# A convolution kernel's engine queues written directly, with one semaphore for all stores and an ending without barriers

## The chip, the cores and the metric

The kernel runs on one core of a Trainium2 chip. The metric is the device time of one execution in microseconds (us). The profile shows a part of it, the *span*, from the program's first instruction to its last. The timed runs list their own spans (all but the first six of the kernel before), so time minus span can be worked out run by run. I call it the *part outside the span*. Most spans are listed to 0.1 us, so this part is good to 0.05 us in a single run. All runs quoted are listed as fast, that is, none is in the slower state in which some runs of a kernel take some per cent longer.

Some words that return: a *semaphore* is a counter that engines and transfers raise and on which an engine can wait. A *barrier* makes engines wait for each other. A *drain* is an instruction that stands ahead of each barrier here. A transfer raises its semaphore in 16 completions (the trace shows 16 for each); it has *landed* with the last of them. The *tail* is the time from the last landing to the end of the span.

## The reference

The input has 8 images of 32 channels and 128 x 128 pixels in float32. The output is `x + conv(groupnorm(x))`, with a 3 x 3 convolution written as an FFT and cut so that only a shifted corner of it is not plain bias:

```python
def reference(x, L0_conv_weight, L0_conv_bias):
    ...
    fx = jnp.fft.fft2(px, norm='ortho')
    fout = jnp.einsum('bihw,oihw->bohw', fx, wf)
    sp = jnp.fft.ifft2(fout, norm='ortho').real
    sh = (fft_H - out_h) // 2
    out = sp[:, :, sh:sh + out_h, sw:sw + out_w]
    ...
    x = x + _L0_conv_ref(_gn(x), L0_conv_weight, L0_conv_bias, 1, 1)
    return x
```

For the timing it is enough to know that 16.8 MB are read and 16.8 MB are written.

## The kernel before

All of x stays on the core, in four tiles of two images each. SyncE issues nine loads and seven stores through one queue. The kernel is written with a framework that keeps track of tiles, gives out semaphores, places the waits, and ends the program by itself when its context is left. These are the parts that the change and the argument touch; cuts are marked.

```python
    pairs = [xpool.tile([P, 2, H, W], F32, name=f"x{pair}") for pair in range(NPAIR)]
    ...
    for img in range(2):
        for half in range(2):
            rows = slice(half * H // 2, (half + 1) * H // 2)
            nc.sync.dma_start(xts[img][:, rows, :], x[0, :, img, rows, :])
            ...
    for pair in range(2, NPAIR):
        nc.sync.dma_start(pairs[pair], x[pair])
    ...
    for img in range(B):
        ...
        if img:
            add(img - 1, 0, NCHUNK)
            if img == 2 or img == 4:
                nc.sync.dma_start(out[img // 2 - 1], pairs[img // 2 - 1])
            elif img > 4:
                store(img - 1, 0, H)
        ...
    store(B - 1, N, H)
    add(B - 1, 0, 2)
    add(B - 1, 2, NCHUNK)
    store(B - 1, 0, N)
...
    with tile.TileContext(nc) as tc, tc.manual_schedule():
        conv_preact_kernel(tc, *args)
```

No line of the source says how the program ends. Leaving the context (L288 in the profile) makes SyncE wait for every semaphore. Then all engines meet in a barrier, GpSimd clears the semaphores, and all engines meet in a second barrier.

## Time and profile before

| what | before | where it is read |
|---|---|---|
| time | 85.69 us (85.48 to 85.76) | three runs |
| profiled run | 85.45 us, span 83.73, so 1.72 outside | its own time and trace |
| 16 DMA engines busy | 95.3% of the span, 99.3% of 2.5 to 82 us | DMA view |
| TensorE busy | 77%, done at 73.5 us | page and timeline |
| last store landed | 82.90 us | semaphore records |
| from there to the end of the span | 0.83 us | the same |

In these numbers the core is a pipe for bytes. It has a short head and a short tail, and the computation lies beside the transfers. The lines themselves are in the prediction.

### The profile page before, as it was taken

To read this page: it belongs to the slowest core of one execution; us is meant where nothing else is said; L and a number is where in the kernel's file an instruction comes from. 1 tells how busy PE (TensorE), PEld (TensorE's weight loads), DVE (VectorE), ACT (ScalarE), POOL (GpSimd) and SP (SyncE) were. 2 spreads that over 40 slices of the span, in tenths; PEclk is the share of its full clock that TensorE was granted. 3 is DMA by queue.
4 is the path that set the end of the run, shared out by engine and by line. 5 is a ranking of instruction groups with operands and counts; after the bars stand their busy time and mean duration, and the time that the engine had idled before them with its cause. 6 is when DMAs were issued, how large, how long until landed. Compare 5 with 4: busy or idle time off the path is not lost.

```text
span 83.7 us, 734 instructions
## 1 busy us (share of the span) xinstructions
PE 64.6 (77%) x214; PEld 39.4 (47%) x214; DVE 54.5 (65%) x103; ACT 51.8 (62%) x102; POOL 2.3 (3%) x8
## 2 busy tenths in 40 slices
PE   0000998999999999999999999999999999900000
PEld 0000441666666666666666666666666666500000
DVE  0329936991999699699969969996996330070000
ACT  6019427984995798499679849967984993000000
POOL 6400000000000000000000000000000000000000
PEclk9999999999999999999999999999999999995555
DMA  2899999999998999899898999899989999999970
GB/s 43 325 407 419 423 450 427 438 431 415 501 501 344 407 501 415 376 438 493 266 485 376 407 470 501 360 407 485 438 352 399 462 407 454 423 446 388 431 335 20
DMA packets 2211, 33.63 MB, mean 402 GB/s; under 512 B 256, under 2 KB 288, under 8 KB 416
## 3 DMA queue, kind: packets, MB, share of 16 engines
q1 hardware_dynamic: 2208, 33.60, 95.3%
q8 instruction: 1, 0.02, 0.1%
q14 instruction: 2, 0.02, 0.1%
HBM read 16.82 MB, written 16.78 MB: 401 GB/s over the span
## 4 chain that ended last, share of the span: by engine, by line
PE 75%; DMA 8%; ACT 2%; DVE 2%; SPq 1%; issue 1%; DVEq 1%
PE ps L189 69%; DMA x<-x_dram 8%; PE ps_w L214 4%; PE ps_m L148 1%; DVE x L198 1%; ACT g L165 1%; DVEq L288 1%; SPq L71 0%; SPq L69 0%; ACT std L160 0%; ACT square L156 0%; ACT rstd L163 0%; DVE rstd L162 0%; DVE var L157 0%
## 5 line engine op out<-in xcount | busy, mean ns | idle before, releaser
L189 PE MATMUL ps<-g,w_sb 128*128 128x363 f32 (+1 forms) x192 | 58.7, 462 | 0.3 <-ACT g L165 0.3
L189 PEld LDWEIGHTS ps<-g,w_sb 128*128 128x128 f32 x192 | 35.2, 189 | 21.2 <-issue 1.9
L129 DVE BATCH_NORM_STATS2 stats<-x 128x6 f32<-128x512 f32 x64 | 38.7, 676 | 2.5 <-DMA x<-x_dram 2.4
L174 ACT ACTIVATE x<-x,bs_sb 128x1984 f32<-128x1984 f32 x8 | 15.6, 1949 | 0.3
L198 DVE SCALAR_TENSOR_TENSOR x<-ps,bs_sb,x 128x1089 f32<-128x1089 f32 (+2 forms) x9 | 10.5, 1179 | 7.2 <-PE ps L189 7.2
L165 ACT ACTIVATE g<-x,rstd 128x396 f32<-128x396 f32 (+1 forms) x16 | 12.6, 837 | 0.3
L214 PE MATMUL ps_w<-x,avg 128*128 128x512 f32 x6 | 5.8, 1100 | 8.5 <-DMA x<-x_dram 8.5
L176 ACT ACTIVATE x<-x,bs_sb 128x1023 f32<-128x1023 f32 x8 | 9.1, 1133 | 0.0
L214 PEld LDWEIGHTS ps_w<-x,avg 128*128 128x128 f32 x6 | 1.7, 326 | 9.6 <-issue 9.6
L156 ACT ACTIVATE square<-ps_m 128x7 f32<-128x7 f32 x8 | 1.4, 176 | 5.5 <-PE ps_m L148 5.5
L139 ACT ACTIVATE terms<-bs_sb,mv 128x8 f32<-128x8 f32 x8 | 2.4, 301 | 3.8 <-DVE mv L137 3.8
L157 DVE COPY var<-ps_m 128x1 f32<-128x1 f32 x8 | 1.3, 158 | 4.9 <-ACT square L156 4.9
L148 PEld LDWEIGHTS ps_m<-terms,avg 128*128 128x128 f32 x16 | 3.2, 205 | 2.7 <-ACT terms L140 1.2
L160 ACT ACTIVATE std<-var 128x1 f32<-128x1 f32 x8 | 2.4, 295 | 1.8 <-DVE var L157 1.8
L163 ACT ACTIVATE rstd<-ps_m,rstd 128x1 f32<-128x1 f32 x8 | 2.1, 261 | 1.8 <-DVE rstd L162 1.8
L162 DVE RECIPROCAL rstd<-std 128x1 f32<-128x1 f32 x8 | 1.3, 164 | 2.9 <-ACT std L160 2.9
L118 ACT ACTIVATE bs_sb<-wb_sb 32x9 f32<-32x9 f32 x4 | 0.8, 211 | 3.8 <-DMA wb_sb<-wb_dram 3.8
L137 DVE BATCH_NORM_AGGREGATE mv<-stats 128x2 f32<-128x48 f32 x8 | 3.0, 372 | 0.3
L121 ACT ACTIVATE w_sb<-wb_sb 32x64 f32<-32x64 f32 (+2 forms) x16 | 2.8, 244 | 0.0
L148 PE MATMUL ps_m<-terms,avg 128*128 128x9 f32 x16 | 2.5, 226 | 0.0
L140 ACT ACTIVATE terms<-mv,eps 128x1 f32<-128x1 f32 x8 | 2.2, 279 | 0.0
L100 ACT ACT_TABLE_LOAD x1 | 1.3, 1283 | 0.8 <-PEq L281 0.8
(14 smaller groups left out, 5.1 us busy)
## 6 DMA issues: line engine op xcount, KB each, us to landing
x<-x_dram SPq DMA_DIRECT2D x2, 4096.0 KB, 33.8
out_dram<-x SPq DMA_DIRECT2D x2, 4096.0 KB, 16.5
out_dram<-x SPq DMA_DIRECT2D x3, 2048.0 KB, 10.2
x<-x_dram SPq DMA_DIRECT2D x4, 1024.0 KB, 7.7
x<-x_dram SPq DMA_DIRECT2D x2, 2048.0 KB, 17.3
out_dram<-x SPq DMA_DIRECT2D x1, 1056.0 KB, 7.9
out_dram<-x SPq DMA_DIRECT2D x1, 992.0 KB, 11.5
wb_sb<-wb_dram SPq DMA_DIRECT2D x1, 40.5 KB, 4.8
```

Source lines behind the costliest of these rows:

```text
L121: nc.scalar.activation(w6[to, dr, dc, r, c, :], taps[:, a, b, :], AF.Identity)
L129: nc.vector.bn_stats(stats[img][:, s, :], xts[img][:, STATS * s : STATS * (s + 1), :].rearrange("p h w -> p (h w)"),)
L137: nc.vector.bn_aggr(mv, stats[img].rearrange("p n s -> p (n s)"))
L139: nc.scalar.activation(terms[:, 0:NSIGN], signs, AF.Identity, scale=mv[:, 0:1])
L148: nc.tensor.matmul(ps_ms[img], avg, mvs[img], start=True, stop=True)
L160: nc.scalar.activation(std, var[:, 0:1], AF.Sqrt, bias=var[:, 1:2])
L165: nc.scalar.activation(g[:, rows, :], xt[:, LO + rows.start : LO + rows.stop, LO:W], AF.Identity, bias=rstd[:, 1:2], scale=rstd[:, 0:1],)
L174: nc.scalar.activation(low, low, AF.Identity, bias=bias_sb)
L176: nc.scalar.activation(right, right, AF.Identity, bias=bias_sb)
L189: nc.tensor.matmul(ps[:, 0:rows, 0 : N - dc], w_sb[:, k * P : (k + 1) * P], g[:, top : top + rows, dc:N], start=(k == 0), stop=(k == 3),)
L198: nc.vector.scalar_tensor_tensor(part.rearrange("p (n r) w -> p n r w", r=ROWS), in0=pss[img][:, first:last, 0 : ROWS * N].rearrange("p n ...
L214: nc.tensor.matmul(ps_w, avg, piece, start=True, stop=True)
```

## The change

The intent is to keep every computing instruction and its order, and to drop what the framework adds. Each engine has one semaphore, which counts its marked instructions. Each load has its own semaphore, and all stores share one. A small class remembers what each engine has already waited for, and leaves out the waits that follow from others. SyncE's wait for the seven stores ends the program. The core of the diff, cut:

```diff
-    with tile.TileContext(nc) as tc, tc.manual_schedule():
-        conv_preact_kernel(tc, *args)
+    conv_preact_kernel(nc, *args)
...
+    def __call__(self, name, emit, *needs, mark=False, adds=None):
+        engine, seen = self.names[name], self.seen[name]
+        waits = {}
+        for token, of in needs:
+            if seen.get(of, 0) < token[of]:
+                waits[of] = max(waits.get(of, 0), token[of])
...
+        for of, value in waits[:-1]:
+            engine.wait_ge(self.sems[of], value)
+        op = emit(engine)
...
-        nc.sync.dma_start(out[img // 2, :, img % 2, first:last, :], xts[img][:, first:last, :])
+    put.semaphore("stored")
+    def store(to, of, *needs):
+        return put("sp", lambda sp: sp.dma_start(to, of), *needs, adds="stored")
...
+    nc.sync.wait_ge(put.sems["stored"], put.done["stored"])
+    numbers = sorted(sem.num for sem in put.sems.values())
+    nc.sync.sem_clear(range(numbers[0], numbers[-1] + 1))
```

More of the change, by code (lines that the diff above doesn't have):

```diff
@@ L18 @@
-from contextlib import ExitStack
 import concourse.bass as bass
-import concourse.tile as tile
 from concourse import mybir
-from concourse._compat import with_exitstack
 F32 = mybir.dt.float32
@@ L34, with __init__, semaphore, _learn @@
 NSIGN = 8
-@with_exitstack
-def conv_preact_kernel(
-    ctx: ExitStack,
-    tc: tile.TileContext,
-    x: bass.AP,
-    wb: bass.AP,
-    out: bass.AP,
-):
-    nc = tc.nc
+LANDED = 16
+class Queues:
+    def __init__(self, nc):
+        self.nc = nc
+        self.names = {"pe": nc.tensor, "dve": nc.vector, "act": nc.scalar, "pool": nc.gpsimd, "sp": nc.sync}
+        self.sems = {}
+        self.done = {}
+        self.seen = {name: {} for name in self.names}
+        for name in self.names:
+            if name != "sp":
+                self.sems[name] = nc.alloc_semaphore(f"done_{name}")
+                self.done[name] = 0
+    def semaphore(self, name):
+        self.sems[name] = self.nc.alloc_semaphore(name)
+        self.done[name] = 0
+    def _learn(self, name, token):
+        for of, value in token.items():
+            self.seen[name][of] = max(self.seen[name].get(of, 0), value)
+    def __call__(self, name, emit, *needs, mark=False, adds=None):
[4 more added lines that the diff above has]
+                waits[of] = max(waits.get(of, 0), token[of])
+        for token, of in needs:
+            self._learn(name, token)
+        waits = list(waits.items())
+        for of, value in waits[:-1]:
+            engine.wait_ge(self.sems[of], value)
+        op = emit(engine)
+        if waits:
+            of, value = waits[-1]
+            op.wait_op(self.sems[of], value, "sem-ge")
+        if adds is not None:
+            of, by = adds, LANDED
+        elif mark:
+            of, by = name, 1
+        else:
+            return None
+        op.then_inc(self.sems[of], by)
+        self.done[of] += by
+        return {**seen, of: self.done[of]}, of
+def conv_preact_kernel(nc: bass.Bass, x: bass.AP, wb: bass.AP, out: bass.AP):
     NPAIR, _, _, H, W = x.shape
@@ L54, in conv_preact_kernel @@
     NSTAT = H // STATS
-    cpool = ctx.enter_context(tc.tile_pool(name="const", bufs=1))
-    xpool = ctx.enter_context(tc.tile_pool(name="x", bufs=1))
-    spool = ctx.enter_context(tc.tile_pool(name="small", bufs=2))
-    ps_conv = ctx.enter_context(tc.tile_pool(name="ps_conv", bufs=2, space=bass.MemoryType.PSUM))
-    ps_stat = ctx.enter_context(tc.tile_pool(name="ps_stat", bufs=1, space=bass.MemoryType.PSUM))
-    pairs = [xpool.tile([P, 2, H, W], F32, name=f"x{pair}") for pair in range(NPAIR)]
@@ L64, in conv_preact_kernel, with sbuf, psum @@
-    xts = [pairs[img // 2][:, img % 2] for img in range(B)]
-    wb_sb = cpool.tile([C, 9 * C + 4 * (1 + NSIGN)], F32, name="wb_sb")
+    def sbuf(name, *shape):
+        return nc.alloc_sbuf_tensor(name, list(shape), F32).ap()
+    def psum(name, *shape):
+        return nc.alloc_psum_tensor(name, list(shape), F32).ap()
+    put = Queues(nc)
+    pairs = [sbuf(f"x{pair}", P, 2, H, W) for pair in range(NPAIR)]
+    xts = [pairs[img // 2][:, img % 2] for img in range(B)]
+    wb_sb = sbuf("wb_sb", C, 9 * C + 4 * (1 + NSIGN))
@@ L66, in conv_preact_kernel, with load @@
+    loaded = {}
+    def load(to, of):
+        name = f"load{len(put.sems)}"
+        put.semaphore(name)
+        return put("sp", lambda sp: sp.dma_start(to, of), adds=name)
     for img in range(2):
+        loaded[img] = []
         for half in range(2):
             rows = slice(half * H // 2, (half + 1) * H // 2)
-            nc.sync.dma_start(xts[img][:, rows, :], x[0, :, img, rows, :])
+            loaded[img].append((rows.stop, load(xts[img][:, rows, :], x[0, :, img, rows, :])))
             if img == 0 and half == 0:
-                nc.sync.dma_start(wb_sb, wb)
+                weights_in = load(wb_sb, wb)
@@ L72, in conv_preact_kernel @@
     for img in range(2):
-        nc.sync.dma_start(xts[2 + img], x[1, :, img])
+        loaded[2 + img] = [(H, load(xts[2 + img], x[1, :, img]))]
     for pair in range(2, NPAIR):
-        nc.sync.dma_start(pairs[pair], x[pair])
-    pair = cpool.tile([P, P // 2, 2], F32, name="pair")
-    nc.gpsimd.memset(pair, 0.125)
-    nc.gpsimd.affine_select(
-        out=pair, in_=pair, pattern=[[-2, P // 2], [0, 2]], base=0,
-        channel_multiplier=1, compare_op=ALU.is_ge, fill=0.0,
-    )
-    nc.gpsimd.affine_select(
-        out=pair, in_=pair, pattern=[[2, P // 2], [0, 2]], base=1,
-        channel_multiplier=-1, compare_op=ALU.is_ge, fill=0.0,
-    )
@@ L88, in conv_preact_kernel @@
-    w_sb = cpool.tile([P, 4 * P], F32, name="w_sb")
-    nc.gpsimd.memset(w_sb, 0.0)
-    eps = cpool.tile([P, 1], F32, name="eps")
-    nc.vector.memset(eps, EPS * FFT * FFT)
-    pair2 = pair.rearrange("p a b -> p (a b)")
-    avg = cpool.tile([P, P], F32, name="avg")
-    nc.vector.tensor_add(avg[:, 0 : 2 * C], pair2[:, 0 : 2 * C], pair2[:, 2 * C : 4 * C])
-    nc.vector.tensor_add(avg[:, 2 * C : 3 * C], avg[:, 0:C], avg[:, C : 2 * C])
-    for k in (0, 1, 3):
-        nc.vector.tensor_copy(avg[:, k * C : (k + 1) * C], avg[:, 2 * C : 3 * C])
@@ L99, in conv_preact_kernel, with rows_in @@
-    warm = cpool.tile([P, 1], F32, name="warm")
-    nc.scalar.activation(warm, eps, AF.Sqrt)
-    bs_sb = cpool.tile([P, 1 + NSIGN], F32, name="bs_sb")
+        loaded[2 * pair] = loaded[2 * pair + 1] = [(H, load(pairs[pair], x[pair]))]
+    def rows_in(img, last):
+        return [token for k, (_, token) in enumerate(loaded[img]) if k == 0 or loaded[img][k - 1][0] < last]
+    pair = sbuf("pair", P, P // 2, 2)
+    w_sb = sbuf("w_sb", P, 4 * P)
+    eps = sbuf("eps", P, 1)
+    avg = sbuf("avg", P, P)
@@ new lines, in conv_preact_kernel @@
+    warm = sbuf("warm", P, 1)
+    pair_ok = put("pool", lambda e: e.memset(pair, 0.125), mark=True)
+    for step, base in ((-1, 0), (1, 1)):
+        pair_ok = put(
+            "pool",
+            lambda e: e.affine_select(
+                out=pair, in_=pair, pattern=[[2 * step, P // 2], [0, 2]], base=base,
+                channel_multiplier=-step, compare_op=ALU.is_ge, fill=0.0,
+            ),
+            pair_ok, mark=True,
+        )
+    w_zero = put("pool", lambda e: e.memset(w_sb, 0.0), mark=True)
@@ new lines, in conv_preact_kernel @@
+    eps_ok = put("dve", lambda e: e.memset(eps, EPS * FFT * FFT), mark=True)
+    pair2 = pair.rearrange("p a b -> p (a b)")
+    sums = put(
+        "dve", lambda e: e.tensor_add(avg[:, 0 : 2 * C], pair2[:, 0 : 2 * C], pair2[:, 2 * C : 4 * C]),
+        pair_ok, mark=True,
+    )
+    sums = put(
+        "dve", lambda e: e.tensor_add(avg[:, 2 * C : 3 * C], avg[:, 0:C], avg[:, C : 2 * C]), sums, mark=True
+    )
+    for k in (0, 1, 3):
+        avg_ok = put(
+            "dve", lambda e: e.tensor_copy(avg[:, k * C : (k + 1) * C], avg[:, 2 * C : 3 * C]), sums, mark=True
+        )
@@ L105, in conv_preact_kernel @@
+    put("act", lambda e: e.activation(warm, eps, AF.Sqrt), eps_ok)
+    bs_sb = sbuf("bs_sb", P, 1 + NSIGN)
     bias_sb, signs = bs_sb[:, 0:1], bs_sb[:, 1:]
@@ L112, in conv_preact_kernel @@
     }
-    for rin in range(2):
-        for cin in range(2):
-            q = 2 * rin + cin
-            to = slice(q * C, (q + 1) * C)
-            of = 9 * C + q * (1 + NSIGN)
-            nc.scalar.activation(bs_sb[to, :], wb_sb[:, of : of + 1 + NSIGN], AF.Identity)
-            for dr, r, a in places[rin]:
-                for dc, c, b in places[cin]:
-                    nc.scalar.activation(w6[to, dr, dc, r, c, :], taps[:, a, b, :], AF.Identity)
-    gs = [cpool.tile([P, N, N], F32, name=f"g{k}") for k in range(2)]
@@ L124, in conv_preact_kernel, with spread @@
-    stats = [cpool.tile([P, NSTAT, 6], F32, name=f"stats{img}") for img in range(B)]
-    mvs, ps_ms, pss = {}, {}, {}
-    def take_stats(img, first, last):
-        for s in range(first, last):
-            nc.vector.bn_stats(
-                stats[img][:, s, :],
-                xts[img][:, STATS * s : STATS * (s + 1), :].rearrange("p h w -> p (h w)"),
+    def spread(to, of):
+        return put("act", lambda e: e.activation(to, of, AF.Identity), weights_in, w_zero, mark=True)
+    for q in range(4):
+        rin, cin = q // 2, q % 2
+        to = slice(q * C, (q + 1) * C)
+        of = 9 * C + q * (1 + NSIGN)
+        bias_ok = spread(bs_sb[to, :], wb_sb[:, of : of + 1 + NSIGN])
+        for dr, r, a in places[rin]:
+            for dc, c, b in places[cin]:
+                w_ok = spread(w6[to, dr, dc, r, c, :], taps[:, a, b, :])
@@ new lines, in conv_preact_kernel @@
+    gs = [sbuf(f"g{k}", P, N, N) for k in range(2)]
+    stats = [sbuf(f"stats{img}", P, NSTAT, 6) for img in range(B)]
+    mvs = [sbuf(f"mv{k}", P, 2) for k in range(B)]
+    terms = [sbuf(f"terms{k}", P, NSIGN + 1) for k in range(B)]
+    squares = [sbuf(f"square{k}", P, NSIGN - 1) for k in range(B)]
+    variances = [sbuf(f"var{k}", P, 2) for k in range(B)]
+    stds = [sbuf(f"std{k}", P, 1) for k in range(B)]
+    rstds = [sbuf(f"rstd{k}", P, 2) for k in range(B)]
+    pss = [psum(f"ps{k}", P, NCHUNK, BANK) for k in range(2)]
@@ new lines, in conv_preact_kernel, with take_stats @@
+    ps_ms = psum("ps_m", P, BANK)
+    ps_w = psum("ps_w", P, BANK)
+    stats_ok, terms_ok, group_ok, means_read, normal, conv_ok, biased, added = {}, {}, {}, {}, {}, {}, {}, {}
+    warm_ok = None
+    def take_stats(img):
+        for s in range(NSTAT):
+            stats_ok[img] = put(
+                "dve",
+                lambda e: e.bn_stats(
+                    stats[img][:, s, :],
+                    xts[img][:, STATS * s : STATS * (s + 1), :].rearrange("p h w -> p (h w)"),
+                ),
+                *rows_in(img, STATS * (s + 1)), mark=s == NSTAT - 1,
@@ L132, in take_stats @@
             )
     def aggregate(img):
-        mv = spool.tile([P, 2], F32, tag="mv", name=f"mv{img}")
-        nc.vector.bn_aggr(mv, stats[img].rearrange("p n s -> p (n s)"))
-        terms = spool.tile([P, NSIGN + 1], F32, tag="terms", name=f"terms{img}")
-        nc.scalar.activation(terms[:, 0:NSIGN], signs, AF.Identity, scale=mv[:, 0:1])
-        nc.scalar.activation(
-            terms[:, NSIGN:], mv[:, 1:2], AF.Identity, bias=eps, scale=float(FFT * FFT)
-        )
-        mvs[img] = terms
@@ L145, in group @@
-    def group(img):
-        ps_ms[img] = ps_stat.tile([P, NSIGN + 1], F32, tag="ps_m", name=f"ps_m{img}")
-        nc.tensor.matmul(ps_ms[img], avg, mvs[img], start=True, stop=True)
-    def normalize(img):
-        xt, g, ps_m = xts[img], gs[img % 2], ps_ms[img]
-        contrasts = ps_m[:, 1:NSIGN]
-        square = spool.tile([P, NSIGN - 1], F32, tag="square", name=f"square{img}")
-        var = spool.tile([P, 2], F32, tag="var", name=f"var{img}")
-        nc.scalar.activation(square, contrasts, AF.Square, accum_out=var[:, 0:1])
-        nc.vector.tensor_copy(var[:, 1:2], ps_m[:, NSIGN:])
-        std = spool.tile([P, 1], F32, tag="std", name=f"std{img}")
-        nc.scalar.activation(std, var[:, 0:1], AF.Sqrt, bias=var[:, 1:2])
-        rstd = spool.tile([P, 2], F32, tag="rstd", name=f"rstd{img}")
-        nc.vector.reciprocal(rstd[:, 0:1], std)
-        nc.scalar.activation(rstd[:, 1:2], ps_m[:, 0:1], AF.Identity, scale=rstd[:, 0:1])
-        for rows in (slice(0, ROWS + 1), slice(ROWS + 1, N)):
-            nc.scalar.activation(
-                g[:, rows, :], xt[:, LO + rows.start : LO + rows.stop, LO:W], AF.Identity,
-                bias=rstd[:, 1:2], scale=rstd[:, 0:1],
@@ new lines, in aggregate @@
+        mv, t = mvs[img], terms[img]
+        mv_ok = put(
+            "dve", lambda e: e.bn_aggr(mv, stats[img].rearrange("p n s -> p (n s)")), stats_ok[img], mark=True
+        )
+        put("act", lambda e: e.activation(t[:, 0:NSIGN], signs, AF.Identity, scale=mv[:, 0:1]), mv_ok, bias_ok)
+        terms_ok[img] = put(
+            "act",
+            lambda e: e.activation(t[:, NSIGN:], mv[:, 1:2], AF.Identity, bias=eps, scale=float(FFT * FFT)),
+            mark=True,
+        )
+    def group(img):
+        group_ok[img] = put(
+            "pe",
+            lambda e: e.matmul(ps_ms[:, 0 : NSIGN + 1], avg, terms[img], start=True, stop=True),
+            terms_ok[img], avg_ok, *means_read.get(img - 1, ()), mark=True,
+        )
@@ new lines, in normalize @@
+    def normalize(img):
+        xt, g, var, std, rstd = xts[img], gs[img % 2], variances[img], stds[img], rstds[img]
+        square_ok = put(
+            "act",
+            lambda e: e.activation(squares[img], ps_ms[:, 1:NSIGN], AF.Square, accum_out=var[:, 0:1]),
+            group_ok[img], mark=True,
+        )
+        copied = put(
+            "dve", lambda e: e.tensor_copy(var[:, 1:2], ps_ms[:, NSIGN : NSIGN + 1]), square_ok, mark=True
+        )
+        std_ok = put(
+            "act", lambda e: e.activation(std, var[:, 0:1], AF.Sqrt, bias=var[:, 1:2]), square_ok, copied, mark=True
+        )
+        rstd_ok = put("dve", lambda e: e.reciprocal(rstd[:, 0:1], std), std_ok, mark=True)
+        shift_ok = put(
+            "act",
+            lambda e: e.activation(rstd[:, 1:2], ps_ms[:, 0:1], AF.Identity, scale=rstd[:, 0:1]),
+            rstd_ok, mark=True,
+        )
+        means_read[img] = (copied, shift_ok)
+        normal[img] = []
+        for rows in (slice(0, ROWS + 1), slice(ROWS + 1, N)):
+            normal[img].append(
+                put(
+                    "act",
+                    lambda e: e.activation(
+                        g[:, rows, :], xt[:, LO + rows.start : LO + rows.stop, LO:W], AF.Identity,
+                        bias=rstd[:, 1:2], scale=rstd[:, 0:1],
+                    ),
+                    shift_ok, *rows_in(img, H), *conv_ok.get(img - 2, ()), mark=True,
+                )
@@ L173, in add_bias @@
         low = xt[:, N:H, :].rearrange("p h w -> p (h w)")
-        nc.scalar.activation(low, low, AF.Identity, bias=bias_sb)
         right = xt[:, 0:N, N:W]
-        nc.scalar.activation(right, right, AF.Identity, bias=bias_sb)
+        free = [*normal[img]] + ([warm_ok] if img == 0 else [])
+        biased[img] = [
+            put("act", lambda e: e.activation(part, part, AF.Identity, bias=bias_sb), *free, mark=True)
+            for part in (low, right)
+        ]
     def multiply(img, n):
         g = gs[img % 2]
-        if n == 0:
-            pss[img] = ps_conv.tile([P, NCHUNK, BANK], F32, tag="ps", name=f"ps{img}")
-        ps = pss[img][:, n, 0 : ROWS * N].rearrange("p (r w) -> p r w", w=N)
+        ps = pss[img % 2][:, n, 0 : ROWS * N].rearrange("p (r w) -> p r w", w=N)
         for k in range(4):
@@ L188, in multiply, with finished @@
             top = n * ROWS + dr
-            nc.tensor.matmul(
-                ps[:, 0:rows, 0 : N - dc], w_sb[:, k * P : (k + 1) * P],
-                g[:, top : top + rows, dc:N],
-                start=(k == 0), stop=(k == 3),
+            needs = [w_ok, normal[img][min(n, 1)]] + added.get(img - 2, [])
+            ok = put(
+                "pe",
+                lambda e: e.matmul(
+                    ps[:, 0:rows, 0 : N - dc], w_sb[:, k * P : (k + 1) * P],
+                    g[:, top : top + rows, dc:N],
+                    start=(k == 0), stop=(k == 3),
+                ),
+                *needs, mark=k == 3,
             )
+        conv_ok[img] = [ok]
     def add(img, first, last):
-        part = xts[img][:, first * ROWS : last * ROWS, 0:N]
-        nc.vector.scalar_tensor_tensor(
-            part.rearrange("p (n r) w -> p n r w", r=ROWS),
-            in0=pss[img][:, first:last, 0 : ROWS * N].rearrange("p n (r w) -> p n r w", w=N),
-            scalar=bias_sb, in1=part.rearrange("p (n r) w -> p n r w", r=ROWS),
-            op0=ALU.add, op1=ALU.add,
-        )
-    def store(img, first, last):
-        nc.sync.dma_start(out[img // 2, :, img % 2, first:last, :], xts[img][:, first:last, :])
-    ps_w = ps_stat.tile([P, BANK], F32, tag="ps_w", name="ps_w")
+        part = xts[img][:, first * ROWS : last * ROWS, 0:N].rearrange("p (n r) w -> p n r w", r=ROWS)
+        ps = pss[img % 2][:, first:last, 0 : ROWS * N].rearrange("p n (r w) -> p n r w", w=N)
+        ok = put(
+            "dve",
+            lambda e: e.scalar_tensor_tensor(part, in0=ps, scalar=bias_sb, in1=part, op0=ALU.add, op1=ALU.add),
+            *conv_ok[img], bias_ok, mark=True,
+        )
+        added.setdefault(img, []).append(ok)
+    put.semaphore("stored")
+    def store(to, of, *needs):
+        return put("sp", lambda sp: sp.dma_start(to, of), *needs, adds="stored")
+    def finished(*imgs):
+        return [token for img in imgs for token in (*biased[img], *added[img])]
     def keep_warm(first, times):
@@ L213, in keep_warm @@
         for _ in range(times):
-            nc.tensor.matmul(ps_w, avg, piece, start=True, stop=True)
+            ok = put(
+                "pe", lambda e: e.matmul(ps_w, avg, piece, start=True, stop=True),
+                avg_ok, *rows_in(0, H), mark=True,
+            )
+        return ok
     keep_warm(H // 2, 2)
-    take_stats(0, 0, NSTAT)
+    take_stats(0)
     aggregate(0)
     group(0)
-    keep_warm(0, 1)
+    warm_ok = keep_warm(0, 1)
     normalize(0)
     add_bias(0)
-    take_stats(1, 0, NSTAT)
+    take_stats(1)
     for img in range(B):
@@ L232, in conv_preact_kernel @@
             if img == 2 or img == 4:
-                nc.sync.dma_start(out[img // 2 - 1], pairs[img // 2 - 1])
+                store(out[img // 2 - 1], pairs[img // 2 - 1], *finished(img - 2, img - 1))
             elif img > 4:
-                store(img - 1, 0, H)
+                store(out[(img - 1) // 2, :, (img - 1) % 2], xts[img - 1], *finished(img - 1))
         if more:
@@ L241, in conv_preact_kernel @@
         if img + 2 < B:
-            take_stats(img + 2, 0, NSTAT)
-    store(B - 1, N, H)
+            take_stats(img + 2)
+    xt, to = xts[B - 1], out[NPAIR - 1, :, 1]
+    store(to[:, N:H, :], xt[:, N:H, :], biased[B - 1][0])
     add(B - 1, 0, 2)
     add(B - 1, 2, NCHUNK)
-    store(B - 1, 0, N)
+    stored = store(to[:, 0:N, :], xt[:, 0:N, :], biased[B - 1][1], *added[B - 1])
+    seen = {**put.seen["sp"]}
+    for of, value in stored[0].items():
+        seen[of] = max(seen.get(of, 0), value)
+    assert all(seen.get(of, 0) == done for of, done in put.done.items()), (seen, put.done)
+    nc.sync.wait_ge(put.sems["stored"], put.done["stored"])
+    numbers = sorted(sem.num for sem in put.sems.values())
+    assert numbers == list(range(numbers[0], numbers[0] + len(numbers)))
+    nc.sync.sem_clear(range(numbers[0], numbers[-1] + 1))
 def kernel(x, L0_conv_weight, L0_conv_bias):
```

## The prediction

> **What bounds the kernel now.** I read the page first, then the DMA view of the long middle stretch, then the lines of the program's first and last barrier, then when each store was issued and landed. The page's header, its DMA rows and its account of the end:
>
> ```profile
> span 83.7 us, 734 instructions
> PE 64.6 (77%) x214; PEld 39.4 (47%) x214; DVE 54.5 (65%) x103; ACT 51.8 (62%) x102; POOL 2.3 (3%) x8
> ...
> PE   0000998999999999999999999999999999900000
> ...
> DMA  2899999999998999899898999899989999999970
> ...
> q1 hardware_dynamic: 2208, 33.60, 95.3%
> ...
> HBM read 16.82 MB, written 16.78 MB: 401 GB/s over the span
> ```
>
> TensorE has no idle slice from the seventh to its last, and the chain of waits gives it 75% of the span; that looks like the bound. But TensorE is done at 73.5 us of 83.7, and the DMA row is full to the last slice but one. Cut to the stretch from 2.5 to 82 us, the DMA view says it more sharply:
>
> ```profile
> DMA packets 2189, 33.47 MB, mean 421 GB/s; under 512 B 253, under 2 KB 285, under 8 KB 413
> ...
> q1 hardware_dynamic: 2186, 33.44, 99.3%
> ```
>
> The 16 DMA engines are 99.3% busy with the kernel's own loads and stores. So the bound is 33.6 MB through one queue, in order: a head before the first byte moves, some 80 us of transfer, and a tail after the last store has landed. TensorE counts only if it makes a store late. The stores, in the views of their two lines:
>
> ```profile
> L206 SPq DMA_DIRECT2D out_dram<-x x5: 332/332/332, 56.7 to 75.0; - x5
> ...
> DMA to landing us min/median/max: 7.9/10.2/11.6
> ...
> L233 SPq DMA_DIRECT2D out_dram<-x x2: 343/345/347, 34.7 to 49.4; - x2
> ...
> DMA to landing us min/median/max: 14.1/16.5/19.0
> ```
>
> The last store is issued at 75.0 us and lands 7.9 later, at 82.9 us, though its 1.06 MB need only 1.06 / 0.43 = 2.5 us at the rate of the middle: it stands in the queue behind the store before it, which the trace's semaphore records land at 80.39. Each store has such a reserve (issue against landing of the transfer ahead): 34.71 and 44.03, 49.38 and 53.74, 56.70 and 63.44, 64.04 and 68.30, 67.79 and 73.15, 68.86 and 78.01, 75.03 and 80.39. The smallest is 4.3 us. Some of it is the delay before a DMA's first byte, which the start shows as below 2 us (issue at 0.80, and the second slice, which ends at 4.2, already at 8 tenths), so compute may slip by some 2 us before the queue runs dry.
>
> What lies behind the last landing is the program's final barrier (L288):
>
> ```profile
> L288 SPq EVENT_SEMAPHORE  x8: 17/28/28, 75.4 to 83.7; - x8
> L288 POOLq EVENT_SEMAPHORE  x4: 17/17/17, 83.1 to 83.6; - x4
> ...
> L288 SPq DRAIN  x3: 7/7/7, 83.0 to 83.3; - x3
> ...
> L288 POOLq EVENT_SEMAPHORE_RANGE_CLEAR  x1: 96/96/96, 83.3 to 83.3; - x1
> ```
>
> In the single instructions: the last landing at 82.90; SyncE's last wait for it 82.92 to 82.95; its drains at 82.99 and 83.04; GpSimd gathers and releases a first barrier at 83.07 and 83.15; the engines leave it about 83.2, drain, GpSimd clears the semaphores at 83.35 and drains at 83.47; a second barrier is gathered at 83.55 and released at 83.63; the last engine leaves at 83.73. That is 83.73 - 82.90 = 0.83 us in which nothing of the problem is done.
>
> **What the Trainium skill says.** "DMA: Bandwidth & Descriptors", section "Anatomy of one DMA — SWDGE (gpsimd) path", gives the variable cost as bytes over 436 GB/s and calls the fixed cost mostly the wait for the write receipt. The middle runs at 421, so I take the 80 us as not to be shortened by any bookkeeping. The same page, "Why a DMA increments its semaphore by 16 and not by 1", warns that two transfers in flight on one semaphore cannot be told apart by partial counts. The new kernel waits only for the sum of all seven stores, 112, and gives each load its own semaphore, so this is sound and needs no extra wait. "Perfetto Trace Analysis", section "Per-engine timelines", says that a sequencer-only instruction shows only its execution, not its wait or the spread of its update. The trace agrees: SyncE's, GpSimd's and the others' instructions of the tail are 7 to 96 ns each, but their handshakes fill 0.83 us; so the tail has to be read from starts, not from durations. "Runtime: NRT & Kernel Launch", section "Instruction fetch mechanics", says that sequencers fetch their streams by DMA of their own, mostly hidden; I come back to that.
>
> **The change, part by part.**
> (1) Tail. Removed: SyncE's waits for each DMA semaphore in turn (all but the last three are passed without waiting, and those three follow the landings), five drains on the path, two barriers through GpSimd. Left: one wait for 112 on the shared semaphore, and one range clear, now on SyncE. The wait still starts 0.02 after the last landing and takes 0.03 (82.95); the next instruction follows 0.04 later, as the first drain does now; the clear takes 0.10, as on GpSimd: 83.09. Saved: 83.73 - 83.09 = 0.64 us, all on the path, since nothing runs beside it.
> (2) Head. The first barrier (L281) stays. The branch into the kernel's block goes. From the end of SyncE's barrier wait (0.73) to its first load (0.80) are 0.065 us; elsewhere SyncE follows a wait with a DMA after 0.037. Saved: 0.03 us, on the path.
> (3) Loads. The last load waits for a semaphore of the first in order to reuse it (1.1 us, issued at 5.85 instead of about 4.75). It gets its own now. Six transfers stand ahead of it, so its data move when they did. Saved: 0.
> (4) Waits of the engines. The instructions that compute are the same in the same order; in the built programs the semaphore-only instructions fall from 18 to 8 on TensorE and from 18 to 7 on SyncE, and rise from 10 to 12 on ScalarE. Small tiles get a buffer per image, so no wait for reuse is added. All of it lies in the reserve of over 2 us before each store. Saved or lost: 0.
> Sum: 0.64 + 0.03 = 0.67 us; 85.69 - 0.67 = 85.02 us, 0.8%.
>
> **The rivals.**
> (a) The measured time is longer than the span: 85.45 against 83.73 in the profiled run, 1.72 us that no view shows. If part of it is what each engine does after its program, four engines now do it early, and only SyncE after the last landing. For it: the final barrier makes all five end together at 83.7. Against: SyncE still has its own share to do, and if that is the longest nothing is gained. It could take off another 0 to 0.5 us: 84.5 to 85.0.
> (b) Instruction fetches. The trace has two of 8 KB at 32 us and one of 16 KB at 39 us:
>
> ```profile
> q8 instruction: 1, 0.02, 0.1%
> q14 instruction: 2, 0.02, 0.1%
> ```
>
> They look like nothing, but they share the DMA engines. The 16 completions of the last load before them come within 0.5 us (22.65 to 23.16). At 32 us two of the 16 trail by 0.5 us and more; from then on three do, and at the end twelve have landed by 81.81 and the last four at 82.26, 82.35, 82.69 and 82.90. The store ends with its slowest engine, so fetches may cost up to 82.90 - 81.81 = 1.1 us. If the shorter streams dropped them all, with (1) and (2) the time would be 83.9; if they fell on one engine, 0.5 worse, 85.5. I expect neither: TensorE's stream only falls from 130 to 116 instructions as built, 107 of which are matmuls that the trace shows as four each, so the streams need the same blocks at nearly the same times.
> (c) An engine is late: the new waits, or one bank for the group means, hold TensorE up. It would need over 2 us before one store. Before, one such buffer is used in the same order, and the waits that replace the old ones name the same producers. At most 86; I give it 1 in 50.
> (d) The tail is hidden anyway, because the clock of the measurement ends elsewhere: then 85.7 and no gain. Against it: the measured time has to contain the wait for the last store, and what follows is serial.
>
> **Range and chances.** The three runs before lie 0.28 us apart (85.48 to 85.76), so half of that is noise on a median. Rival (a) and the good side of (b) widen the range downward to 84.4, the bad side of (b) and (d) upward to 85.5. More than 2% faster is below 83.98: it needs all of (b), or much of (a) and (b) together; I give that 6%. Slower by over 2% would be over 87.4, for which nothing speaks: 1%.
>
> **What would show it.** Right: the span falls to about 83.0, the last landing stays at 82.9 within a few tenths, one wait and one clear follow it within 0.2 us, the DMA share of the middle stays at 99%. If the span falls by 0.7 and the time by clearly more, (a) holds. If the last landing itself moves by over 0.4 us, look at the fetch rows and at the spread of the 16 completions: (b). If the DMA row shows a hole before a store, (c). Wrong altogether is the argument if the landing stays, the tail is gone, and the time does not move.

## The result, and the profile after

The changed kernel took 84.43 us (83.91 to 84.66, 6 runs), beside 85.72 (85.48 to 85.78, 6 runs) for the kernel before. Ratios here are the mean time of one kernel's fast runs over that of the other's in the same rounds, so not quite the ratio of the medians quoted. This ratio is 0.985 (95% interval 0.981 to 0.988). The gain is 1.3 us, where 0.7 was forecast. The page of the changed kernel:

```profile
span 82.9 us, 697 instructions
...
PE 65.0 (78%) x214; PEld 39.4 (47%) x214; DVE 54.5 (66%) x103; ACT 52.0 (63%) x102; POOL 2.3 (3%) x8
...
PE   0000999999999999999999999999999999950000
...
DMA  2899999999996997999889998998999999999991
...
q1 hardware_dynamic: 2208, 33.60, 96.1%
q8 instruction: 1, 0.02, 0.1%
q14 instruction: 2, 0.02, 0.1%
```

The work of the engines is the same, and so are the bytes. The span is 0.79 us shorter. In the DMA row the end shows it, where the last two slices read 91 instead of 70; the other slices differ by one or two tenths in both directions. The stretch from 2.5 to 82 us, in the DMA view:

```profile
DMA packets 2190, 33.48 MB, mean 421 GB/s; under 512 B 253, under 2 KB 285, under 8 KB 413
...
q1 hardware_dynamic: 2187, 33.45, 99.3%
```

It has the same rate and the same share as before. The stores, and then the ending, each in the view of its line:

```profile
L320 SPq DMA_DIRECT2D out_dram<-x x7: 332/333/445, 34.5 to 75.2; - x7
...
DMA to landing us min/median/max: 7.7/11.3/19.2
```

```profile
L376 SPq EVENT_SEMAPHORE_RANGE_CLEAR  x1: 55/55/55, 82.9 to 82.9; - x1
```

The last store is issued at 75.2 us, a little later than before, and lands at the same time: 82.87 us, against 82.90. It waits in the queue either way. The eight waits, the drains, the gathers and the releases of the old ending have become one instruction. The clear carries the wait for the stores itself, starts 0.02 us after the landing and takes 0.055. The tail is 0.07 us instead of 0.83.

So the tail explains 0.76 of the span's 0.79 us, and the landing 0.03. The rest of the gain, some 0.5 us, is not in any view of the span. In the six runs the time minus the span is 1.21 to 1.29 us (1.25 in the profiled run, whose span is known more finely); the profiled run of the kernel before had 1.72. The experiments ask what the ending has to do with that part.

### The profile page after: what moved, and what is told of

It is laid out like the page before. It is cut to its first block, busy times and chain, and to the rows that moved or that the text cites. A ratio compares the mean times of both kernels' runs of the same rounds, so it can differ in the third digit from the quotient of the medians.

```text
span 82.9 us, 697 instructions
## 1 busy us (share of the span) xinstructions
PE 65.0 (78%) x214; PEld 39.4 (47%) x214; DVE 54.5 (66%) x103; ACT 52.0 (63%) x102; POOL 2.3 (3%) x8
## 4 chain that ended last, share of the span: by engine, by line
PE 76%; DMA 8%; DVE 2%; ACT 2%; SPq 1%; issue 1%
PE ps L297 70%; DMA x<-x_dram 8%; PE ps_w L330 5%; DVE x L312 2%; PE ps_m L234 1%; SPq L117 1%; ACT g L266 1%; ACT std L252 0%; ACT square L243 0%; ACT rstd L257 0%; DVE rstd L254 0%; DVE var L248 0%
## 5 line engine op out<-in xcount | busy, mean ns | idle before, releaser
L281 ACT ACTIVATE x<-x,bs_sb 128x1984 f32<-128x1984 f32 (+1 forms) x16 | 23.9, 1543 | 0.3
L266 ACT ACTIVATE g<-x,rstd 128x396 f32<-128x396 f32 (+1 forms) x16 | 12.7, 840 | 0.3
L243 ACT ACTIVATION_READ_ACCUMULATOR square<-ps_m 128x1 f32 x8 | 1.6, 196 | 0.0
```

The lines of the kernel that those rows point to most:

```text
L243: lambda e: e.activation(squares[img], ps_ms[:, 1:NSIGN], AF.Square, accum_out=var[:, 0:1]),
L266: lambda e: e.activation(g[:, rows, :], xt[:, LO + rows.start : LO + rows.stop, LO:W], AF.Identity, bias=rstd[:, 1:2], scale=rstd[:, 0:1],),
L281: put("act", lambda e: e.activation(part, part, AF.Identity, bias=bias_sb), *free, mark=True)
```

## The experiments

Twelve kernels ran. Each starts from the changed kernel unless it says otherwise, and each was timed beside the kernel before on the same chip. All gave right results, except one. Its output is wrong, which doesn't matter for the time.

### The old ending put back (e1_barriers)

```diff
     nc.sync.wait_ge(put.sems["stored"], put.done["stored"])
-    nc.sync.sem_clear(range(numbers[0], numbers[-1] + 1))
+    nc.all_engine_barrier()
+    nc.gpsimd.sem_clear(range(numbers[0], numbers[-1] + 1))
+    nc.all_engine_barrier()
```

> The changed kernel with the old ending put back behind SyncE's wait: barrier, clear on GpSimd, barrier. The changed kernel took 84.43 us, of which 1.21 to 1.26 us lie outside its span in all six runs; the kernel before took 85.45 with 1.72 outside. Theory A (a part of the gain lies outside the span, because four engines end early): span 0.7 to 0.8 us longer, outside back at 1.7, time 85.6 to 85.8, ratio to before 1.00. Rival B (the outside part comes from the shorter program or the missing branches): outside stays at 1.25, time 85.1 to 85.3, ratio 0.995.

It took 85.89 us (ratio to the kernel before 0.997, 0.993 to 1.001). The part outside the span was 1.69 to 1.75 us. From the views of its two barriers' lines:

```profile
L376 SPq DRAIN x1: 7/7/7, 83.7 to 83.7; - x1
...
L378 POOLq EVENT_SEMAPHORE  x2: 17/17/17, 84.1 to 84.2; - x2
...
L378 PEldq EVENT_SEMAPHORE  x1: 51/51/51, 84.2 to 84.2; - x1
```

From SyncE's drain at 83.66 to the last engine's leaving at 84.27 are 0.6 us, made of instructions of 7 to 114 ns. The landing was at 83.59, so the tail was 0.68 us. That this landing is 0.7 us later than before is not the ending's doing: one of the 16 completions is 0.87 us behind the others from the load that lands at 9.17 us on, with no fetch in the trace near it, and over the six runs the spans (83.9 to 84.4) match those of the kernel before (83.8 to 84.8). With the ending alone put back, both the tail and the outside part return, and with them nearly all of the gain is gone. Own semaphores, fewer waits and the direct queues are all still in this kernel, so they earned little or nothing (the interval leaves up to 0.6 us). Theory A holds and rival B falls.

### All five engines end late, without a barrier (e2_hold_four)

```diff
+    held = [put.names[name] for name in ['pe', 'act', 'dve', 'pool']]
+    put.semaphore("gone")
+    for engine in held:
+        engine.wait_ge(put.sems["stored"], put.done["stored"]).then_inc(put.sems["gone"], 1)
     nc.sync.wait_ge(put.sems["stored"], put.done["stored"])
+    nc.sync.wait_ge(put.sems["gone"], len(held))
```

> The changed kernel, in which TensorE, ScalarE, VectorE and GpSimd also wait for the last landing and tell SyncE, which clears after that: all five end together, but without a barrier. Theory A: the part outside the span goes back to 1.7 us, and the span grows by one hop (0.1 to 0.2 us): 85.0 to 85.1 us. Rival B: outside stays at 1.25, time 84.5 to 84.7.

It took 84.99 us (ratio 0.988, 0.984 to 0.992), with 1.63 to 1.70 us outside the span. The views of its ending's lines:

```profile
L376 POOLq EVENT_SEMAPHORE  x1: 17/17/17, 83.0 to 83.0; - x1
```

```profile
L381 SPq EVENT_SEMAPHORE_RANGE_CLEAR  x1: 52/52/52, 83.2 to 83.2; - x1
```

This kernel has no barrier, and GpSimd has nothing to clear. The four engines only wait for the landing before they end. That alone brings back 0.4 us outside the span, as theory A says. Which of them causes it is the next question.

### Each engine as the last one (x_pe, x_act, x_dve, x_pool)

Here the wait for the stores and the clear are given to another engine, and SyncE ends with the issue of its last store. The edit of x_pool is shown; the other three name their own engine in its place:

```diff
-    nc.sync.wait_ge(put.sems["stored"], put.done["stored"])
+    last = put.names["pool"]
+    last.wait_ge(put.sems["stored"], put.done["stored"])
...
-    nc.sync.sem_clear(range(numbers[0], numbers[-1] + 1))
+    last.sem_clear(range(numbers[0], numbers[-1] + 1))
```

> The changed kernel, whose last wait and clear stand on TensorE instead of SyncE; SyncE is done at 75 us. With SyncE last, 1.21 to 1.33 us lie outside the span (12 runs of two kernels); with all five last, 1.63 to 1.70. Theory A1 (each engine has work of its own after the program, of different length, and the slowest of those that end late sets the outside part): outside is some number for each of the four engines and reaches about 1.65 for at least one of them. Rival A2 (it is the number of engines that end together, who then wait for each other): outside is 1.25 or below for each one alone.

> The same with ScalarE last. A1: a number between 0.9 and 1.7 of its own, the highest of the four being about 1.65. A2: 1.25 or below.

> The same with VectorE last. A1: a number between 0.9 and 1.7 of its own, the highest of the four being about 1.65. A2: 1.25 or below.

> The same with GpSimd last, which also clears, as in the kernel before. A1: a number of its own; I hold GpSimd for the most likely one to reach 1.65. A2: 1.25 or below. The span in all four runs should be that of the changed kernel, 82.7 to 83.6, as the tail after the last landing stays at about 0.1.

| engine that ends last | outside the span, us | runs |
|---|---|---|
| SyncE (changed kernel) | 1.21 to 1.29 | 6 |
| VectorE | 1.37 to 1.39 | 4 |
| ScalarE | 1.38 to 1.42 | 4 |
| TensorE | 1.48 to 1.60 | 4 |
| GpSimd | 1.81 to 1.84 | 4 |

The medians of the times were 84.82 (TensorE), 84.78 (ScalarE), 84.63 (VectorE) and 85.33 us (GpSimd). The spans were 83.0 to 84.0, not 82.7 to 83.6 as expected, and the tails 0.12 to 0.18, so the times tell less than the parts outside. A1 holds in its main point: the length depends on which engine ends last. A2 falls, as each of the four alone is above 1.25. VectorE and ScalarE are too close to be told apart. The highest is 1.82, not my 1.65. I had taken 1.65 from e2_hold_four, where GpSimd's last instruction ended 0.18 us before SyncE's (83.07 and 83.24), so 1.82 - 0.18 = 1.64 was to be seen there (measured 1.66). The same sum fits the kernel before. GpSimd's release of its second barrier ends at 83.64 us, 0.09 before the span's end, and 1.82 - 0.09 = 1.73 (measured 1.72). It also fits e1_barriers: 84.18 and 84.27, so again 1.73 (measured 1.72 on average). The clear on GpSimd, for comparison, as its line's view has it:

```profile
L377 POOLq EVENT_SEMAPHORE_RANGE_CLEAR  x1: 114/114/114, 83.2 to 83.2; - x1
```

On SyncE it takes 50 to 61 ns. What an engine does in its outside part, no record shows. The runs show its length alone, and that SyncE's is the shortest.

### One semaphore for each store (e3_own_sems)

```diff
-    put.semaphore("stored")
+    stores = []
...
+        put.semaphore(f"stored{len(stores)}")
+        stores.append(f"stored{len(stores)}")
-        return put("sp", lambda sp: sp.dma_start(to, of), *needs, adds="stored")
+        return put("sp", lambda sp: sp.dma_start(to, of), *needs, adds=stores[-1])
...
-    nc.sync.wait_ge(put.sems["stored"], put.done["stored"])
+    for name in stores:
+        nc.sync.wait_ge(put.sems[name], put.done[name])
```

> The changed kernel with one semaphore for each store and seven waits on SyncE at the end. My theory: sharing the semaphore gives nothing, as six of the seven waits are over before the last landing: same time as the changed kernel, 84.3 to 84.6, tail after the last landing 0.1 us. Rival: the six other waits are paid after the landing, at 0.05 us each: 0.3 us more.

It took 84.48 us (ratio 0.983, 0.978 to 0.987), and its tail was 0.15 us. SyncE's own waits show why it is so close:

```profile
SPq L376 <- DMA out_dram<-x: 7.5, 3, 2.7
```

The three waits add up to 7.5 us, with 2.7 us the longest. They follow the last three landings one by one, and all but the last are over when the last store lands. Sharing one semaphore saves the difference of the tails, 0.15 - 0.07 = 0.08 us, which no timing of these runs resolves.

### The first load ahead of the first barrier (e4_early_load)

After the program is recorded, SyncE's first load is moved before its barrier drain; the other eight stay where they are:

```diff
     conv_preact_kernel(nc, *args)
+    body = nc.main_func.blocks[0]
+    order = list(body.instructions)
+    sync = [i for i in order if i.engine == mybir.EngineType.SP]
+    load = next(i for i in sync if i.opcode == "DMACopy")
+    barrier = next(i for i in sync if i.opcode == "Drain")
+    order.remove(load)
+    order.insert(order.index(barrier), load)
+    body.instructions = order
```

> The changed kernel with SyncE's first load (1 MB) issued before the first barrier, at about 0.05 us of the span instead of 0.80; the others stay behind it. If the one queue bounds the kernel from its first byte to its last, all that follows comes 0.7 us earlier: 83.7 us, ratio to before 0.976. Rival: the end hangs on the chain of compute or on a fixed fetch of instructions, and the time stays at 84.4, or only the head moves and the span grows less short, by 0.3 or below.

It took 83.58 us (83.39 to 84.01), with a ratio of 0.971 (0.967 to 0.975). The loads' line, first in this run and then in the changed kernel:

```profile
L117 SPq DMA_DIRECT2D x<-x_dram x8: 377/432/942, 0.0 to 4.0; - x8
```

```profile
L117 SPq DMA_DIRECT2D x<-x_dram x8: 383/472/506, 0.8 to 4.8; - x8
```

The first packet moves at 1.00 us instead of 1.83, and both span and time come out 0.9 us shorter than those of e3_own_sems in the same rounds (medians of six: span 82.3 and 83.25, time 83.58 and 84.48). The 0.2 us beyond the 0.7 expected can be the longer tail of e3_own_sems (0.08) and the first packet, which came 0.83 us earlier and not 0.7; they are also within what the runs of one kernel differ by. The profiled execution, one of the two slower ones of the six, shows less: its last landing is at 82.65 us, only 0.22 earlier than in the changed kernel, as the completions of its last store spread over 2.0 us instead of 1.7. The claim rests on the six runs. The outside part stays (1.21 to 1.29). So the queue does bound the kernel from its first byte to its last, and what is taken from the head comes off the time. This kernel beats both.

### The changed kernel again (after_again)

No edit.

> The changed kernel once more, beside the kernel before on the same chip, to have spans of both: if the gain is the tail (0.76 us in the profiles) and the part outside the span (about 0.5), the median span is 0.7 to 0.9 us shorter, the outside part 1.2 to 1.3, the time 1.2 to 1.6 us shorter, the more of it the oftener the kernel before shows 2.0 outside instead of 1.7.

It took 84.64 us (ratio 0.985, 0.980 to 0.991). The means of the same rounds give the account of the gain: 86.04 us before, as 84.16 of span and 1.88 outside, and 84.74 after, as 83.48 and 1.26. Of the 1.30 us, 0.68 are span and 0.62 are outside it. The span's share is the tail (0.76 in the profiles), less what the landing differed by chance. Of the outside share, 1.72 - 1.26 = 0.46 is the change of the last engine. The other 0.16 has another source. In 6 of these 11 runs the kernel before shows 1.97 to 2.05 outside, and in the rest 1.69 to 1.77.

### The branches put back (b_branches)

The two levels of the kernel before were still open: e1_barriers, with the same ending, never showed the upper one. It lacks the branches between the blocks of the program. This kernel is e1_barriers with

```diff
+    nc.br("kernel_body")
+    nc.switch_bb("kernel_body")
...
+    nc.br("kernel_end")
+    nc.switch_bb("kernel_end")
     nc.all_engine_barrier()
```

> The kernel with the old ending (run e1_barriers, outside part 1.69 to 1.75 in all six runs) with the two branches of the kernel before put back on every engine, one behind the first barrier and one ahead of the ending. The kernel before shows two levels outside its span, 1.7 and 2.0, in 13 runs near 1.7 or 1.8 and 15 near 2.0 of three calls (29 runs, one of them 1.78). Theory C (the branches make the second level): this kernel shows 2.0 in about half of its runs, and its mean is that of the kernel before, ratio 1.00. Rival: it shows 1.7 in all six runs, and the second level has another source; the ratio stays at 0.997. Head: if the branch at the start costs 0.03 us, SyncE's first load starts that much later than 0.80.

It took 85.71 us (ratio 1.001, 0.997 to 1.005), with 1.67 to 1.80 outside in all six runs. Theory C finds no support. But the kernel before, on this chip, showed the upper level in only 1 of 11 runs, so six runs cannot exclude it either. Where the second level comes from stays open. The run does settle the head: with the branch, SyncE's first load starts at 0.801 us, and without it, in the changed kernel, at 0.803. The branch costs nothing that shows.

### More instruction fetches (n_pool700)

The spread of the last store's completions suggested that instruction fetches hold up single DMA engines. GpSimd has no work after 3 us, so it can be given instructions that nothing waits for:

```diff
     w_zero = put("pool", lambda e: e.memset(w_sb, 0.0), mark=True)
+    idle = sbuf("idle", P, 700)
+    for k in range(700):
+        nc.gpsimd.memset(idle[:, k : k + 1], 0.0)
```

> The changed kernel with 700 more instructions on GpSimd (each sets one column of a scratch tile) after its own setup; nothing waits for them, and GpSimd is otherwise idle. Theory F (instruction fetches take turns on the DMA engines and the slowest engine sets the last landing): more instruction packets appear in the DMA view, at least 2 of 16 KB, the spread of the last store's 16 completions grows and the last landing comes 0.3 to 2 us later. Rival: fetches are hidden, the last landing stays within 82.6 to 83.4 us.

It took 87.22 us (86.97 to 87.36), with a ratio of 1.013 (1.009 to 1.018). The line of these instructions, and the queues in the DMA view:

```profile
L154 POOL MEMSET idle<- x700: 98/99/101, 3.0 to 30.2; 128x1 f32 x175
```

```profile
q1 hardware_dynamic: 2208, 33.60, 93.2%
q14 instruction: 8, 0.07, 0.2%
q8 instruction: 1, 0.02, 0.1%
```

The 700 instructions end at 30 us, and no instruction needs what they write. Still, the last landing is at 85.86 us, and the kernel is 2.6 us slower than after_again; I had expected 0.3 to 2 us. Row q14 has six packets of 8 KB more than before (my expectation said 16 KB). They are at 7.7, 12.7, 17.9, 22.9, 28.4 us and one among three at 32 to 34 us. The 16 completions of the loads then spread further with each: 0.7 us for the load that lands at 11, 1.3 at 14, 2.0 at 20, 2.7 at 25. That is about 0.65 us per fetch, on one engine: in the last three of these loads the other 15 completions stay within 0.35 us. Each of the last three steps holds one fetch, though the loads land 3 to 6 us apart, so the steps follow the fetches and not the time for which the instructions ran. At the end, all other completions of the stores are in by 83.34 us, and the last comes at 85.86. Fetches that take 0.2% of the DMA time can set the end of a kernel that is bound by the queue, since a transfer ends with its slowest engine. GpSimd itself stood still, too, 4.0 us in five gaps, each of which begins 0.4 to 1.3 us after the start of one of the first five fetches.

A rival has to be looked at: VectorE was late in this run as well. The line of its three small copies at 3 us, from the page:

```profile
L166 DVE COPY avg<-avg 128x32 f32<-128x32 f32 x3 | 6.0, 5885 | 0.0
```

They take 0.18 us each in the changed kernel. Here they end at 9.0 to 9.1 us, when GpSimd's first stretch of these instructions stops (8.98). TensorE starts 0.76 us later, and the last store is issued at 75.80 us instead of 75.04 in after_again. That did not make the stores late: each was issued 2.1 us or more before the first engine had finished the transfer ahead of it (64.72 against 66.79), and at the start 1.0 us passed from issue to first packet.

### A quarter of the matmuls, results wrong (t_one_tap)

```diff
-        for k in range(4):
+        for k in (0,):
...
-                    start=(k == 0), stop=(k == 3),
+                    start=True, stop=True,
```

> The changed kernel with one of the four matmuls of each chunk: its results are wrong on purpose; loads and stores are the same. TensorE's stream falls from 437 to about 150 instructions and its time to a quarter. Queue-bound theory: no gain from TensorE's 45 us less work; the time is that of the changed kernel within 0.3 us. Theory F adds: the 16 KB fetch at 40 us goes, and the last landing may come up to 0.3 us earlier. Rival (TensorE bounds the kernel): the time falls by several us.

It took 84.94 us (ratio 0.987, 0.982 to 0.992); after_again, in the same rounds, took 84.64. The relative error of its results is 0.02, as taps are missing. The page:

```profile
PE 41.0 (49%) x70; PEld 17.4 (21%) x70; DVE 54.5 (65%) x103; ACT 51.8 (62%) x102; POOL 2.3 (3%) x8
...
PEclk9999999985555555555555555555555558955555
...
q1 hardware_dynamic: 2208, 33.60, 95.6%
q14 instruction: 2, 0.02, 0.1%
```

TensorE has a third as many instructions, and the time does not fall. TensorE was in the way of nothing, although it led the chain of waits with 75% of the span. Its busy time falls only to 41.0 us, not to a quarter: a matmul took 825 ns on average instead of 464, at a granted clock of half for most of the run. The fetch of 16 KB on q8 is gone, as theory F said, but the last landing did not come earlier: it was at 83.45 us in the profile. So the runs show no gain from dropping that fetch, and the part of theory F about it found no support. It is not refuted either, because in this profile another delay of the same size took its place. Between the load that lands at 33.5 us and the one at 44.6 the spread of the completions grew from 1.2 to 2.2 us without any fetch in the trace. What holds that engine up there is open, as it is in e1_barriers.

## Why the prediction was right or wrong

**What bounds the kernel** was right. The queue-bound reading is confirmed from both sides: e4_early_load took 0.9 us off by starting the queue earlier, and t_one_tap took away two thirds of TensorE's instructions for nothing.

**Part (1), the tail,** had the right mechanism and was sized a little low: 0.64 us forecast, 0.76 measured. I had counted a wait, a gap and a clear of 0.10 us. The wait rides on the clear itself, and SyncE clears in 0.055. The error of part (2) goes the other way and hides 0.03 of this in the sum.

**Part (2), the head,** was wrong, by little: 0.03 forecast, 0.00 measured. The gap after the barrier is there with the branch and without it.

**Parts (3) and (4), loads and waits,** were right. The last load is issued at 4.75 instead of 5.85 us and lands at 43.98 instead of 44.03. All the stores are issued within 0.2 us of the old times. (The reserve of 4.3 us was counted to the last of a transfer's 16 completions; the first engine was done 1.6 us sooner, so the true reserve was smaller. No run came to its end.) With all of it left in, but the old ending put back, the gain is gone.

**Rival (a) is the step that failed.** The prediction wrote "It could take off another 0 to 0.5 us" and then took 0 into its sum, with the reason "SyncE still has its own share to do, and if that is the longest nothing is gained". SyncE's share is not the longest but the shortest of the five, 1.25 us against 1.82 of GpSimd, which ended the old program 0.09 us before the last engine. So the part outside fell from 1.72 to 1.26. That is 0.46 us, near the upper end of the rival's own range, and it belonged in the sum: 0.76 + 0.46 = 1.2 of the 1.3 us. The prediction's own sign for it came true: the span fell by some 0.7, and the time by clearly more. I could have seen from the page that GpSimd, ScalarE and TensorE are idle at the end, but no view of the kernel before tells what each engine costs after its program. The right forecast from what was known was a point in the middle of the rival's range, not at its lower end. The rest, some 0.1 us, is within the difference of the landings and the second level of the kernel before.

**Rival (b)** was right as forecast: the same three fetches (at 31.96, 32.08 and 40.39 us; before at 31.94, 32.08 and 39.18), and no gain from them. That fetches can delay the last store is shown by n_pool700; that those three cause the spread of the unchanged kernel is not shown, and t_one_tap gives no support for the third. **Rivals (c) and (d)** did not occur.

**The page on DMA.** The section that the prediction names for the rate describes transfers that GpSimd issues; here SyncE issues them all. The argument needs only the measured rate, which is 421 GB/s before and after.

## What to carry to other kernels

When one queue bounds a kernel, look at what stands before its first byte and after its last landing: here the old ending, two barriers and a clear, cost 0.76 us more in the span than the new one, and a first load ahead of the opening barrier won another 0.9. Let the engine that ends soonest after its program be the one that waits for the last store, and let the others finish early; compare time minus span from run to run, since that part is in no view. And keep the instruction streams of idle engines short while the queue is full. Still open are what an engine does in its part outside the span, where the second level of the kernel before comes from, and what holds up single DMA engines where no fetch shows.

## What the Trainium skill lacked or had wrong

- "Runtime: NRT & Kernel Launch", section "The ~15µs preamble/postamble breakdown", gives one postamble for the program (barrier about 1.5 us, semaphore reset about 1.5 us, another barrier with the reset of the DMA rings about 2 us). No run shows whether the part outside the span holds these stages. The page does not say that it matters which engine ends last. The runs show 1.25 us outside the span with SyncE last, 1.38 with VectorE, 1.40 with ScalarE, 1.54 with TensorE and 1.82 with GpSimd.
- "Runtime: NRT & Kernel Launch", section "Instruction fetch mechanics", calls the cost of a fetch mostly hidden, and blocks of 16 KiB the unit. In n_pool700 the further fetches came as single packets of 8 KB (the fetch on q8 as one of 16 KB). The slowest DMA engine fell about 0.65 us further behind with each of three that can be told apart, the kernel with six more of them was 2.6 us slower, and the fetching engine stood still for 4.0 us in five gaps.
- No page has what a program's own two barriers with a clear between them cost at its end (the runtime page has only those that the runtime adds): 0.68 us after the last landing in e1_barriers, 0.83 in the kernel before.
